# A graph network on one core: half-size stretches of the count matrix, one-hots of their own for the seam matmul, and the first block's counts fetched during the build

## The chip, the core and the metric

The kernel runs on 1 core of one Trainium2 chip. The metric is device time in microseconds (us). TensorE is called PE below, its weight loads PEld, VectorE DVE, ScalarE ACT, GpSimd POOL, and SyncE SP; a "q" behind the name (SPq, PEldq) marks that engine's own instruction sequencer, where DMA issues and register loads stand.

## The reference, cut to what matters

Two graph layers over 6250 nodes with 128 features and 200000 edges that are sorted by destination:

```python
h = jnp.maximum(_layernorm(x, axis=-1), 0.0)
# layer 0: agg_src = segment_sum(h[src], dst); agg_edge = segment_sum(edge_attr, dst)
x = x + relu(concatenate([h, agg_src, agg_edge], axis=1) @ W.T + b)
h = jnp.maximum(_layernorm(x, axis=-1), 0.0)
# layers 1 and 2 (mean over the neighbours, the same edges)
h1 = relu(mean(h[src]) @ W1_l + b1 + h @ W1_r)
out = x + relu(mean(h1[src]) @ W2_l + b2 + h1 @ W2_r)
```

## The kernel before

The kernel never gathers rows. It builds once a matrix `counts_d` in DRAM that says how many edges lead from each source node to each destination node, and then does each of the three layers as a dense matmul with it. Nodes are cut into NB = 49 blocks of 128; `counts_d` has 128 rows (source modulo 128), and for each destination node 49 bf16 columns (source block), so a destination block of 128 nodes is 12544 bytes a row, 1568 KB in all.

**The build.** Edges are taken in 196 groups of 1024, a group in 8 tiles of 128 edges. A tile's counts are a product of two one-hot matrices: `sp` (source modulo 128) stands, `sq` (destination place times 49 plus source block) moves. DVE writes both for a whole group by comparing an iota with an index (`onehots`, L391); PE multiplies (L504) into a PSUM tile `pu`; ACT copies the product into an SBUF buffer `ring` at a place that is read from a list (`to_put`, L531). Since edges are sorted, a tile touches a narrow window of `w` destination nodes. `REGIONS` says for each 14 groups: tiles per window `n`, window `w`, groups per stretch `k`, nodes of a stretch `sw`, window of the edge sums. Groups of one stretch share one `ring` buffer (three in rotation, each of SWMAX = 148 nodes, 14504 bytes a partition). At a stretch's end SP writes the whole ring to `counts_d` (L559) at a column that it reads from the list `first_i`; these writes overlap one another, and each is ordered behind the one before.

Where two windows meet they can share a node. For n > 1 (the first 84 groups) POOL adds the first 49 columns of a window to the ring (L534), and at the start of a stretch copies 49 columns over from the ring before (L481). For n = 1 (the last 112 groups, from group G1 = 84) PE does it: each tile's product gets a second matmul (L516) with the edges of the tile before, whose `sq` is read at an offset that a register holds:

```python
step = steps[t0 if t0 != live[0] else 0]
for j0, (sp_b, sq_b, t) in enumerate(last_tiles):
    mm = nc.tensor.matmul(pu[:, i * 512 : i * 512 + NB], sp_b[:, t, :],
                          sq_b[:, t, bass.ds(step, NB)], start=False, ...)
```

The 8 offsets of a group come from the list `step_i`, by one register load on PE's sequencer in each group (`group_values`, its load has the line L384); ACT loads its 8 places from `at_i` in the same way, once in each group.

Woven into this, PE sums the edges' features: `edge_sums` loads 512 KB of edges (SP, L403, three buffers), makes a one-hot `hot` (L405), multiplies (L414, fp32), and DVE adds the sum to `aggE` (L419) at a place read from `first_i`. The 196 edge groups are spread so that 1.27 of them fall on each group with n = 1. Every third group also gets one block of layer 0's linear part (`first_layer`), up to block 48.

**The layers.** When the build's pools are closed, 49 destination blocks follow for each layer (`neighbours`): SP loads the block's counts into `c` (L578, 1568 KB, three buffers in the pool `loads`, which takes the SBUF that the build had), PE runs 49 matmuls (L584), DVE reduces and finishes, ACT and PE make the next layer's terms (`next_layer`). For every second block DVE also takes the largest count (`high` L592, `worse` L593). `windows_right` tests on the fly that the windows held all edges: POOL loads the lists into `both`, `nexts` and `rows`, and DVE works over them (L642 to L689). In the program it is called from the second layer's loop.

The order of instructions on each engine is not the program's: a list scheduler chooses it ahead of the run, by the dependences and by its own estimate of durations. So work that nothing holds back, as these tests, can be moved far ahead.

Of the kernel before, what the change touches and what calls it, by code (L numbers as in the profile page):

```python
# [9 lines left out]
F32 = mybir.dt.float32  # L10
F16 = mybir.dt.float16
BF16 = mybir.dt.bfloat16
I32 = mybir.dt.int32
AF = mybir.ActivationFunctionType
ALU = mybir.AluOpType
AX = mybir.AxisListType
ET = mybir.EngineType
# [17 lines left out]

REGIONS = (
    (4, 4, 14, 40, 8),
    (4, 6, 14, 110, 12),
    (2, 5, 7, 100, 18),
    (2, 7, 7, 134, 22),  # L40
    (2, 8, 2, 60, 28),
    (2, 9, 2, 70, 32),
    (1, 6, 2, 74, 36),
    (1, 7, 2, 86, 42),
    (1, 8, 2, 98, 46),
    (1, 9, 2, 106, 52),
    (1, 10, 2, 118, 56),
    (1, 10, 2, 128, 62),
    (1, 11, 2, 140, 68),
    (1, 12, 2, 148, 74),  # L50
)
SWMAX = 148
WINMAX = 74


# [1 line left out]
def kernel(ctx: ExitStack, tc: tile.TileContext, x, srcl, dstl, edge, w0t, b0, w1l, b1, w1r, w2l, b2, w2r, out):  # L57
# [31 lines left out]
    for g0, g1, *reg in regions:  # L89
        for g in range(g0, g1, reg[2]):  # L90
            stretches.append((g, min(reg[2], g1 - g), *reg))
    NS = len(stretches)

    dram = ctx.enter_context(tc.tile_pool(name="dram", bufs=1, space=bass.MemoryType.DRAM))
    counts_d = dram.tile([P, (NP + SWMAX) * NB], BF16, name="counts_d")
# [25 lines left out]
    first = const.tile([P, 2, G], F32, name="first")  # L121
    terms = [keep.tile([P, NB, TW], BF16, name="terms0")]
    aggE = keep.tile([P, NP + WINMAX], F32, name="aggE")

    build = ExitStack()
    lists = build.enter_context(tc.tile_pool(name="lists", bufs=1))
# [3 lines left out]
    at_i = lists.tile([1, GC * U], I32, name="at_i")  # L130
    first_i = lists.tile([1, G], I32, name="first_i")
    G1 = next(g for g, _, n, *_ in stretches if n == 1)
    step_i = lists.tile([1, (G - G1) * U], I32, name="step_i")
    seam_i = lists.tile([1, NS], I32, name="seam_i")
    NQ = max(w for _, _, _, w, *_ in regions) * NB
    iota = lists.tile([P, NQ + NQ % 2], F16, name="iota")
# [140 lines left out]
    while si < NS:  # L277
# [21 lines left out]
    nc.vector.tensor_tensor(seam[:, 1:], seam[:, 1:], most[:, : NS - 1], op=ALU.min)  # L299
    nc.vector.tensor_scalar(seam, seam, 0.0, float(NB), op0=ALU.max, op1=ALU.mult)  # L300
    nc.vector.tensor_copy(seam_i, seam)
    steps = room.rearrange("o g u -> o (g u)")[:, : (G - G1) * U]
    nc.vector.tensor_tensor(steps, flat(unit)[:, G1 * U :], flat(unit)[:, G1 * U - 1 : GU - 1], op=ALU.subtract)
    nc.vector.tensor_scalar(
        steps, steps, float(max(r[3] for r in regions) - 1), float(NB), op0=ALU.min, op1=ALU.mult
    )
    nc.vector.tensor_scalar(step_i, steps, 0.0, None, op0=ALU.max)

    nc.sync.dma_start(unit_d[1 : GU + 1].unsqueeze(0), flat(unit))
    for end, u in ((0, 0), (GU + 1, GU - 1)):  # L310
# [4 lines left out]

    nc.vector.tensor_scalar(
        bad[:, 1:2], starts[:, NS - 1 : NS], -1.0, float(NC * P - stretches[-1][5]), op0=ALU.mult, op1=ALU.add
    )
    setup.close()
    nc.gpsimd.memset(terms[0][:, :, NK * D :], 1.0)  # L320
# [62 lines left out]
    def group_values(ap, engine, most):  # L383
        _, values = nc.values_load_multi_w_load_instructions(  # L384
            ap, engines=[engine], min_val=0, max_val=most, skip_runtime_bounds_check_because="clamped on the chip"
        )
        return values

    def onehots(to, index, n, m):
# [5 lines left out]
            op=ALU.is_equal,  # L395
        )

    def edge_sums(g):

        win = win_of(g)  # L400
        e = edges.tile([P, U, D], F32, name="edge_t")
        at_e = min(g * EG, E - EG)
        nc.sync.dma_start(e, edge[at_e : at_e + EG, :].rearrange("(p u) f -> p u f", u=U))  # L403
        hot = padded[g % len(padded)]
        nc.vector.tensor_tensor(  # L405
            hot[:, :, :win],
            iota[:, :win].unsqueeze(1).to_broadcast([P, U, win]),
            rel[:, g, :].unsqueeze(2).to_broadcast([P, U, win]),
            op=ALU.is_equal,
        )  # L410
        ps = bpsum.tile([P, 512], F32, name="pe", bufs=2)
        for u in range(U):
            behind = yield
            mm = nc.tensor.matmul(ps[:, :P], e[:, u, :], hot[:, u, :], start=u == 0, stop=u == U - 1)  # L414
            if behind is not None:
                tc.add_manual_dep(mm.ins, behind.name, IN_ORDER, reason="in turn with the counts")
        base = value(first_i[0:1, g : g + 1], ET.DVE, N - 1)
        to = aggE[:, bass.ds(base, win)]
        nc.vector.tensor_tensor(to, to, ps[:, :win], op=ALU.add)  # L419

    def all_edge_sums():
        for g in range(G):
            yield from edge_sums(g)

    edge_tiles = all_edge_sums()
    next(edge_tiles)
# [40 lines left out]
    before = None  # L467
    counted = None
    writes = []
    steps_of = {}  # L470
    block = 0
    for i in range(2):
        load_chunk(i)
    for si, (g0, ng, n, w, k, sw, win) in enumerate(stretches):
# [4 lines left out]
        if before is not None and n > 1:  # L479
            v = value(seam_i[0:1, si : si + 1], ET.Pool, (SWMAX - 1) * NB)  # L480
            nc.gpsimd.tensor_copy(ring[:, :NB], before[:, bass.ds(v, NB)])  # L481
        for g in range(g0, g0 + ng):
            sp = hots.tile([P, U, P], BF16, name="sp")
            onehots(sp, p_e[:, g], U, P)
            even = nq + nq % 2
# [4 lines left out]
            if n > 1:  # L490
                to_add = group_values(places, ET.Pool, (sw - w) * NB)
            else:
                steps = steps_of.pop(g)
            live = [t for t in range(0, U, n) if g < G - 1 or (t + n) * P > unused]
            many = 2 if nq <= 512 else 1
            for j in range(0, len(live), many):
                units = live[j : j + many]
                pu = bpsum.tile([P, 2 * 512], F32, name="pu", bufs=3)
                for i, t0 in enumerate(units):
                    for t in range(t0, t0 + n):  # L500
                        c = i * 512
                        while c < i * 512 + nq:
                            z = min(c // 512 * 512 + 512, i * 512 + nq)
                            mm = nc.tensor.matmul(  # L504
                                pu[:, c:z],
                                sp[:, t, :],
                                sq[:, t, c - i * 512 : z - i * 512],
                                start=t == t0,
                                stop=t == t0 + n - 1 and (n > 1 or c > i * 512),
                            )  # L510
                            c = z
                    if n == 1:

                        step = steps[t0 if t0 != live[0] else 0]
                        for j0, (sp_b, sq_b, t) in enumerate(last_tiles):
                            mm = nc.tensor.matmul(  # L516
                                pu[:, i * 512 : i * 512 + NB],
                                sp_b[:, t, :],
                                sq_b[:, t, bass.ds(step, NB)],
                                start=False,  # L520
                                stop=j0 == len(last_tiles) - 1,
                            )
                    last_tiles = [(sp, sq, t) for t in range(t0, t0 + n)]
                if n > 1:
                    fore = small.tile([P, 2, NB], F32, name="fore", bufs=8)
                    nc.scalar.copy(  # L526
                        fore[:, : len(units), :], pu.rearrange("p (i c) -> p i c", c=512)[:, : len(units), :NB]
                    )
                for i, t0 in enumerate(units):
                    if n == 1:  # L530
                        nc.scalar.copy(ring[:, bass.ds(to_put[t0], nq)], pu[:, i * 512 : i * 512 + nq])  # L531
                        continue
                    to = ring[:, bass.ds(to_add[t0 // n], NB)]
                    add = nc.gpsimd.tensor_tensor(to, to, fore[:, i, :], op=ALU.add)  # L534
                    tc.add_to_no_dep_group(f"add{si}", add.ins)
                    put = nc.scalar.copy(  # L536
                        ring[:, bass.ds(to_put[t0 // n] + NB, nq - NB)], pu[:, i * 512 + NB : i * 512 + nq]
                    )

                    tc.declare_no_dep(put.ins, group=f"add{si}", reason="a later window's other nodes stand behind it")  # L540
                spent += share(n) * len(units) / len(live)
                sum_edges(min(int(spent / shares * GU + 0.5), GU), counted)
                counted = mm.ins
                if j == 0 and G1 <= g + 1 < G:

                    steps_of[g + 1] = group_values(
                        step_i[0:1, (g + 1 - G1) * U : (g + 2 - G1) * U], ET.PE, (max(r[3] for r in regions) - 1) * NB
                    )

            if len(writes) > 1 or block == NB and writes:  # L550
                writes.pop(0)()
# [5 lines left out]
        else:  # L557
            begin = value(first_i[0:1, g0 : g0 + 1], ET.SP, N - 1) * NB
        nc.sync.dma_start(counts_d[:, bass.ds(begin, sw * NB)], ring[:, : sw * NB])  # L559
        before = ring  # L560
    assert block == NB and summed == GU and not writes
    build.close()
# [9 lines left out]
    def neighbours(layer, b):  # L572
# [1 line left out]
        ps = psum.tile([P, 512], F32, name="ps", bufs=3)  # L574
        m = NK * D + (layer == 0)
        products = []
        c = loads.tile([P, P, NB], BF16, name="c")
        nc.sync.dma_start(c, counts_d[:, b * P * NB : (b + 1) * P * NB].rearrange("p (d k) -> p d k", k=NB))  # L578
        for k in range(NB):
            products.append((c[:, :, k], terms[layer % 2][:, k, :m]))  # L580
        for i, (stands, moves) in enumerate(products):
# [26 lines left out]
    def windows_right():  # L608

        both = late.tile([P, 2, GU], F32, name="both")  # L610
        dst, far = both[:, 0], both[:, 1]
        nc.gpsimd.dma_start(dst.bitcast(I32), dstl)
        nexts = late.tile([P, GU], I32, name="nexts")
        nc.gpsimd.memset(nexts[P - 32 :, GU - U :], PAD)
        nc.gpsimd.dma_start(nexts[: P - 1, :], dstl[1:, :])
        nc.gpsimd.dma_start(nexts[P - 1 :, : GU - U], dstl[0:1, U:])
# [361 lines left out]
```

## Time and profile before

| | us |
|---|---|
| median of 3 runs (2259.93 to 2263.4) | 2262.35 |
| the profiled execution: its own time | 2267.7 |
| the profiled execution: span from first to last instruction | 2266.0 |
| busy: PE / DVE / ACT / POOL | 2067.5 / 1207.9 / 791.9 / 217.9 |
| stage with n > 1 | about 48 to 319 |
| stage with n = 1 | 319 to 934 |
| first matmul of layer 0 | 947.16 |
| layers 0, 1, 2 | 947 to 1405, to 1850, to 2266 |

The mean granted clock of TensorE was 0.982. Busy time is the union of an engine's instructions; the ends of matmuls are modelled, so small gaps of PE are not all seen. "Idle before" names what ended the idle time of an engine; "issue" means that nothing the profile follows ended it, and a register load on the engine's own sequencer is such a case.

### The profile page before, as it was taken

To read this page: it belongs to the slowest core of one execution; us is meant where nothing else is said; L and a number is where in the kernel's file an instruction comes from. 1 tells how busy PE (TensorE), PEld (TensorE's weight loads), DVE (VectorE), ACT (ScalarE), POOL (GpSimd) and SP (SyncE) were. 2 spreads that over 40 slices of the span, in tenths; PEclk is the share of its full clock that TensorE was granted. 3 is DMA by queue.
4 is the path that set the end of the run, shared out by engine and by line. 5 is a ranking of instruction groups with operands and counts; after the bars stand their busy time and mean duration, and the time that the engine had idled before them with its cause. 6 is when DMAs were issued, how large, how long until landed. Compare 5 with 4: busy or idle time off the path is not lost.

```text
span 2266.0 us, 39466 instructions
## 1 busy us (share of the span) xinstructions
PE 2067.5 (91%) x13713; PEld 1693.1 (75%) x13713; DVE 1207.9 (53%) x2296; ACT 791.9 (35%) x2010; POOL 217.9 (10%) x421
## 2 busy tenths in 40 slices
PE   6977778898888888779999999999999999999998
PEld 5865557777666666567888887778888888888887
DVE  8987765677666666475555555444444431111111
ACT  3565566788888787311111111111111110000000
POOL 5666650000000000100000000000000000000000
PEclk9999999999999999899999999999999999999999
DMA  3554566777777677745555555555555556666663
GB/s 116 187 170 166 187 222 227 254 273 263 250 254 266 243 257 258 271 157 205 209 204 202 200 199 196 180 192 186 191 204 191 185 200 218 228 227 229 226 226 135
DMA packets 140315, 478.93 MB, mean 211 GB/s; under 512 B 15249, under 2 KB 85967, under 8 KB 114384
## 3 DMA queue, kind: packets, MB, share of 16 engines
q1 hardware_dynamic: 81540, 447.53, 55.5%
q10 hardware_dynamic: 57996, 27.16, 4.2%
q8 instruction: 115, 1.88, 0.3%
q0 software_dynamic: 576, 1.63, 0.2%
q14 instruction: 88, 0.72, 0.1%
HBM read 362.19 MB, written 114.08 MB: 210 GB/s over the span
## 4 chain that ended last, share of the span: by engine, by line
PE 61%; issue 10%; DVE 10%; DMA 9%; ACT 6%; ACTq 2%; POOLq 1%; POOL 1%; DVEq 0%; SPq 0%
PE ps L584 37%; PE pe L414 12%; PE pu L504 7%; DMA c<-counts_d 6%; ACT ring L531 3%; PE pz L344 2%; DVE high L592 2%; DVE sq L391 1%; DVE worse L593 1%; PE pu L516 1%; ACTq L384 1%; DMA edge_t<-in_edge 1%; PE pt L341 1%; ACT ring L536 1%; ACT h L334 1%
## 5 line engine op out<-in xcount | busy, mean ns | idle before, releaser
L584 PE MATMUL ps<-terms,c 128*128 128x384 bf16 (+1 forms) x7203 | 1228.3, 327 | 13.1 <-DMA c<-counts_d 13.1
L584 PEld LDWEIGHTS <-c 128*128 128x128 bf16 x7203 | 1020.5, 142 | 180.6 <-issue 18.8
L414 PE MATMUL pe<-hot,edge_t 128*128 128x128 f32 x3136 | 517.9, 294 | 19.9 <-DMA edge_t<-in_edge 12.8
L531 ACT CAST ring<-pu 128x490 f32 (+6 forms) x891 | 470.3, 534 | 108.2 <-PE pu L516 69.9
L414 PEld LDWEIGHTS pe<-hot,edge_t 128*128 128x128 f32 x3136 | 419.0, 195 | 78.6 <-issue 32.3
L504 PE MATMUL pu<-sq,sp 128*128 128x512 bf16 (+7 forms) x1782 | 396.3, 315 | 34.1 <-ACT ring L536 16.1
L391 DVE TENSOR_TENSOR sq<-iota,q_e 128x3136 bf16<-128x3136 f16 (+8 forms) x196 | 353.2, 1802 | 0.0
L595 DVE TENSOR_REDUCE y<-ps 128x128 f32<-128x384 f32 x147 | 81.2, 553 | 384.7 <-PE ps L584 384.7
L504 PEld LDWEIGHTS <-sp 128*128 128x128 bf16 x1782 | 176.3, 100 | 140.5 <-issue 84.2
L391 DVE TENSOR_TENSOR sp<-iota,p_e 128x1024 bf16<-128x1024 f16 x196 | 136.2, 695 | 172.3 <-PE pu L516 154.8
L516 PE MATMUL pu<-sq,sp 128*128 x892 | 163.5, 186 | 64.4 <-issue 63.6
L534 POOL TENSOR_TENSOR ring<-ring,fore 128x49 f32 x280 | 173.5, 620 | 89.9 <-ACT fore L526 30.3
L593 DVE TENSOR_REDUCE worse<-high 128x1 f32<-128x3136 bf16 x49 | 167.5, 3419 | 1.6
L347 DVE TENSOR_TENSOR r<-pz,b_sb 128x128 f32<-128x128 f32 x98 | 28.6, 292 | 226.8 <-ACT terms L345 226.8
L536 ACT CAST ring<-pu 128x196 f32 (+5 forms) x280 | 112.0, 404 | 71.9 <-issue 34.9
L330 ACT ACTIVATE rstd<-mv,eps 128x1 f32<-128x1 f32 x98 | 29.0, 300 | 287.2 <-DVE mv L328 287.2
L516 PEld LDWEIGHTS <-sp 128*128 128x128 bf16 x892 | 87.4, 98 | 43.2 <-issue 12.6
L732 ACT ACTIVATE h<-y 128x128 f32<-128x128 f32 x49 | 15.1, 309 | 289.4 <-DVE y L724 289.4
L592 DVE TENSOR_TENSOR high<-c 128x3136 bf16<-128x3136 bf16 x49 | 87.7, 1790 | 49.4 <-DMA c<-counts_d 49.1
L405 DVE TENSOR_TENSOR hot<-iota,rel 128x64 f32<-128x64 f16 (+13 forms) x196 | 96.0, 492 | 0.6 <-POOL hot L375 0.6
L350 ACT CAST terms<-z 128x128 bf16<-128x128 f32 x147 | 44.0, 300 | 92.9 <-DVE z L349 92.1
L351 DVE TENSOR_TENSOR terms<-z,terms 128x128 bf16<-128x128 f32 x147 | 44.2, 301 | 59.6 <-ACT terms L350 59.3
(138 smaller groups left out, 820.7 us busy)
## 6 DMA issues: line engine op xcount, KB each, us to landing
c<-counts_d SPq DMA_DIRECT2D x147, 1568.0 KB, 6.4
edge_t<-in_edge SPq DMA_DIRECT2D x196, 512.0 KB, 3.7
counts_d<-ring SPq DMA_DIRECT2D x7, 1813.0 KB, 6.2
counts_d<-ring SPq DMA_DIRECT2D x7, 1715.0 KB, 6.5
counts_d<-ring SPq DMA_DIRECT2D x7, 1568.0 KB, 6.7
counts_d<-ring SPq DMA_DIRECT2D x7, 1445.5 KB, 5.7
own<-r_d ACTq DMA_DIRECT2D x147, 64.0 KB, 5.5
counts_d<-ring SPq DMA_DIRECT2D x7, 1298.5 KB, 6.2
```

What stands on the lines that cost most here:

```text
L391: nc.vector.tensor_tensor(to.rearrange("p t (c two) -> p t c two", two=2), iota[:, :m].rearrange("p (c two) -> p c two", two=2).unsqueeze( ...
L405: nc.vector.tensor_tensor(hot[:, :, :win], iota[:, :win].unsqueeze(1).to_broadcast([P, U, win]), rel[:, g, :].unsqueeze(2).to_broadcast([P ...
L414: mm = nc.tensor.matmul(ps[:, :P], e[:, u, :], hot[:, u, :], start=u == 0, stop=u == U - 1)
L504: mm = nc.tensor.matmul(pu[:, c:z], sp[:, t, :], sq[:, t, c - i * 512 : z - i * 512], start=t == t0, stop=t == t0 + n - 1 and (n > 1 or c ...
L516: mm = nc.tensor.matmul(pu[:, i * 512 : i * 512 + NB], sp_b[:, t, :], sq_b[:, t, bass.ds(step, NB)], start=False, stop=j0 == len(last_tile ...
L531: nc.scalar.copy(ring[:, bass.ds(to_put[t0], nq)], pu[:, i * 512 : i * 512 + nq])
L534: add = nc.gpsimd.tensor_tensor(to, to, fore[:, i, :], op=ALU.add)
L536: put = nc.scalar.copy(ring[:, bass.ds(to_put[t0 // n] + NB, nq - NB)], pu[:, i * 512 + NB : i * 512 + nq])
L584: nc.tensor.matmul(ps[:, :m], stands, moves, start=i == 0, stop=i == len(products) - 1)
L592: nc.vector.tensor_tensor(high, cf[:, :half], cf[:, half:], op=ALU.max)
L593: nc.vector.tensor_reduce(worse[:, 6 + b : 7 + b], high, AX.X, ALU.max)
L595: nc.vector.tensor_reduce(y, ps[:, : NK * D].rearrange("p (k f) -> p f k", k=NK), AX.X, ALU.add)
```

## The change

Four things are done.

The stretches get shorter. In regions 1, 2 and 3 a stretch has 7, 4 and 3 groups in place of 14, 7 and 7, and in the last six regions 1 group in place of 2; `sw` goes down with it and SWMAX from 148 to 86. The number of stretches, and so of ring writes, goes from 76 to 124.

The seam matmul of n = 1 gets one-hots of its own. `carries` works out once, at group 14, an index `carry` for each tile (the index of the edges less the step); for each group DVE writes `sc` from it, 9 tiles of 50 columns at most, and L516 reads `sc` at a fixed place. The register load of `step_i` on PE is gone.

A buffer `c_early` (12544 bytes a partition) is kept from the start. POOL loads block 0's counts into it for layer 0 once all but the last 6 stretches are written; a further entry of `bad` tests that those 6 do not reach block 0. In the layers, each fourth block (b % 4 == 0) uses `c_early` and no buffer of `loads`.

The tests of the lists are tied to layer 0: POOL copies a column of `rdeg` of block 12 into `dst`, and one of block 16 into `nexts`, before it loads them.

```diff
 REGIONS = (
     (4, 4, 14, 40, 8),
-    (4, 6, 14, 110, 12),
-    (2, 5, 7, 100, 18),
-    (2, 7, 7, 134, 22),
+    (4, 6, 7, 70, 12),
+    (2, 5, 4, 62, 18),
+    (2, 7, 3, 66, 22),
     (2, 8, 2, 60, 28),
...
-    (1, 8, 2, 98, 46),
-    (1, 9, 2, 106, 52),
-    (1, 10, 2, 118, 56),
-    (1, 10, 2, 128, 62),
-    (1, 11, 2, 140, 68),
-    (1, 12, 2, 148, 74),
+    (1, 8, 1, 54, 46),
+    (1, 9, 1, 60, 52),
+    (1, 10, 1, 68, 56),
+    (1, 10, 1, 72, 62),
+    (1, 11, 1, 76, 68),
+    (1, 12, 1, 82, 74),
 )
-SWMAX = 148
+SWMAX = 86
...
+    EARLY = NS - 6
...
+    c_early = keep.tile([P, P, NB], BF16, name="c_early")
...
+    nc.vector.tensor_scalar(
+        bad[:, 3:4], starts[:, EARLY : EARLY + 1], -1.0, float(P), op0=ALU.mult, op1=ALU.add
+    )
...
+    def carries():
+        ones = small.tile([1, P], F32, name="ones", bufs=1)
+        nc.vector.memset(ones, 1.0)
...
+        for i in range(2):
+            nc.tensor.matmul(
+                pu[:, i * 512 : i * 512 + half], ones, steps[:, i * half : (i + 1) * half], start=True, stop=True
+            )
+            nc.vector.tensor_tensor(
+                carry[:, 1 + i * half : 1 + (i + 1) * half],
+                flat_q[:, T1 - 1 + i * half : T1 - 1 + (i + 1) * half],
+                pu[:, i * 512 : i * 512 + half].unsqueeze(2).to_broadcast([P, half, 2]),
+                op=ALU.subtract,
+            )
...
         for g in range(g0, g0 + ng):
+            if g == RUN:
+                carries()
...
             else:
-                steps = steps_of.pop(g)
+                of_first = 2 if g == G1 else 1
+                sc = hots.tile([P, U + 1, NB + NB % 2], BF16, name="sc")
+                c0 = g * U - T1 + 1
+                onehots(
+                    sc[:, 2 - of_first : U + 1], carry[:, c0 + 1 - of_first : c0 + U], U + of_first - 1, NB + NB % 2
+                )
...
-                                sq_b[:, t, bass.ds(step, NB)],
+                                sc[:, slot + 1 - len(last_tiles) + j0, :NB],
...
-                if j == 0 and G1 <= g + 1 < G:
-                    steps_of[g + 1] = group_values(
-                        step_i[0:1, (g + 1 - G1) * U : (g + 2 - G1) * U], ET.PE, (max(r[3] for r in regions) - 1) * NB
-                    )
...
         nc.sync.dma_start(counts_d[:, bass.ds(begin, sw * NB)], ring[:, : sw * NB])
+        if si == EARLY - 1:
+            load_counts(nc.gpsimd, c_early, 0)
...
-        c = loads.tile([P, P, NB], BF16, name="c")
-        nc.sync.dma_start(c, counts_d[:, b * P * NB : (b + 1) * P * NB].rearrange("p (d k) -> p d k", k=NB))
+        c = c_early if b % 4 == 0 else loads.tile([P, P, NB], BF16, name="c")
+        if b or layer:
+            load_counts(nc.sync, c, b)
...
+        nc.gpsimd.tensor_copy(dst[:, 0:1], rdeg[:, 12:13])
         nc.gpsimd.dma_start(dst.bitcast(I32), dstl)
         nexts = late.tile([P, GU], I32, name="nexts")
+        nc.gpsimd.tensor_copy(nexts[:, 0:1], rdeg[:, 16:17])
```

More of the change, by code (lines that the diff above doesn't have):

```diff
@@ L132 @@
     G1 = next(g for g, _, n, *_ in stretches if n == 1)
-    step_i = lists.tile([1, (G - G1) * U], I32, name="step_i")
+    T1 = G1 * U
+    carry = lists.tile([P, GU - T1 + 1, 2], F16, name="carry")
+    steps = lists.tile([1, GU - T1], F32, name="steps")
     seam_i = lists.tile([1, NS], I32, name="seam_i")
@@ L301 @@
     nc.vector.tensor_copy(seam_i, seam)
-    steps = room.rearrange("o g u -> o (g u)")[:, : (G - G1) * U]
-    nc.vector.tensor_tensor(steps, flat(unit)[:, G1 * U :], flat(unit)[:, G1 * U - 1 : GU - 1], op=ALU.subtract)
+    nc.vector.tensor_tensor(steps, flat(unit)[:, T1:], flat(unit)[:, T1 - 1 : GU - 1], op=ALU.subtract)
     nc.vector.tensor_scalar(
-        steps, steps, float(max(r[3] for r in regions) - 1), float(NB), op0=ALU.min, op1=ALU.mult
+        steps, steps, float(max(r[3] for r in regions)), float(NB), op0=ALU.min, op1=ALU.mult
     )
-    nc.vector.tensor_scalar(step_i, steps, 0.0, None, op0=ALU.max)
     nc.sync.dma_start(unit_d[1 : GU + 1].unsqueeze(0), flat(unit))
@@ L396, in onehots @@
         )
+    def carries():
+        ones = small.tile([1, P], F32, name="ones", bufs=1)
+        nc.vector.memset(ones, 1.0)
+        flat_q = q_e.rearrange("p g u two -> p (g u) two")
+        pu = bpsum.tile([P, 2 * 512], F32, name="pu", bufs=3)
+        half = (GU - T1) // 2
+        assert half <= 512 and 2 * half == GU - T1
+        for i in range(2):
[8 more added lines that the diff above has]
+            )
+        nc.vector.tensor_tensor(
+            carry[:, 0:1], flat_q[:, T1 - 2 : T1 - 1], pu[:, 0:1].unsqueeze(2).to_broadcast([P, 1, 2]), op=ALU.subtract
+        )
     def edge_sums(g):
@@ L423, in all_edge_sums, with load_counts @@
             yield from edge_sums(g)
+    def load_counts(queue, c, b):
+        queue.dma_start(c, counts_d[:, b * P * NB : (b + 1) * P * NB].rearrange("p (d k) -> p d k", k=NB))
     edge_tiles = all_edge_sums()
@@ L469 @@
     writes = []
-    steps_of = {}
     block = 0
@@ L492 @@
             else:
-                steps = steps_of.pop(g)
+                of_first = 2 if g == G1 else 1
[3 more added lines that the diff above has]
+                    sc[:, 2 - of_first : U + 1], carry[:, c0 + 1 - of_first : c0 + U], U + of_first - 1, NB + NB % 2
+                )
             live = [t for t in range(0, U, n) if g < G - 1 or (t + n) * P > unused]
@@ L512 @@
                     if n == 1:
-                        step = steps[t0 if t0 != live[0] else 0]
-                        for j0, (sp_b, sq_b, t) in enumerate(last_tiles):
+                        slot = t0 + 1 if t0 != live[0] else 1
+                        for j0, (sp_b, t) in enumerate(last_tiles):
                             mm = nc.tensor.matmul(
@@ L522 @@
                             )
-                    last_tiles = [(sp, sq, t) for t in range(t0, t0 + n)]
+                    last_tiles = [(sp, t) for t in range(t0, t0 + n)]
                 if n > 1:
```

## The prediction

> **What bounds the kernel now.** I read the busy rows by stage first, then the waits of the stage that the change rewrites, then single instructions inside it, and last the passage from the build to layer 0. In the layers (947 to 2266 us) PE is the bound: between 1100 and 2266 it is busy for 1143.5 of 1166 us, so little can be gained there. The idle time is in the build. By region of 14 groups (last region, and the sum over the last six; columns: length, then busy time and count of PE, PEld, DVE, ACT, POOL, then clock, DMA share, GB/s):
>
> ```profile
> 848.00:934.10 86.10, 73.51 (x598) 57.20 (x596) 54.38 (x58) 69.17 (x108) 3.12 (x1) 0.98 0.68 246
> sum 472.60, PE 412.39 PEld 322.52 DVE 315.60 ACT 385.81 POOL 3.33; mean PE 68.73 PEld 53.75 DVE 52.60 ACT 64.30 POOL 0.55
> ```
>
> Those 84 groups take 5.63 us each, and PE is idle for 60.2 of the 472.6 us. The waits of 319 to 934 say where (engine, line, what it waited for: total us, times, longest):
>
> ```profile
> DVE sp L391 <- PE pu L516: 154.8, 93, 4.6
> ACT ring L531 <- PE pu L516: 69.9, 89, 2.1
> ...
> PE pu L516 <- issue: 63.6, 65, 2.8
> ```
>
> PE stops before the seam matmul L516 with nothing visible to wait for, and ACT and DVE then stop for PE. What stands there is the register load of `step_i`. Two group ends in a row, with SP's issues around them:
>
> ```profile
> L384 PEldq TENSOR_LOAD <-step_i x1: 1697/1697/1697, 804.5 to 804.5; - x1
> L384 ACTq TENSOR_LOAD <-at_i x1: 1626/1626/1626, 805.2 to 805.2; - x1
> ```
>
> ```profile
> L384 ACTq TENSOR_LOAD <-at_i x1: 547/547/547, 810.9 to 810.9; - x1
> L384 PEldq TENSOR_LOAD <-step_i x1: 589/589/589, 810.9 to 810.9; - x1
> ```
>
> ```profile
> 800.63 0.35 SPq L559 DMA_DIRECT2D counts_d<-ring  x1
> 803.92 5.89 SPq L403 DMA_DIRECT2D edge_t<-in_edge  x2
> 813.07 0.35 SPq L559 DMA_DIRECT2D counts_d<-ring  x1
> ```
>
> The loads at 804.5 and 805.2 fall 4 to 6 us after a ring write was issued, and take 1.7 and 1.6 us; those at 810.9 have no write in flight and take 0.59 and 0.55. Writes of this size land late, so every second group end is a slow one:
>
> ```profile
> counts_d<-ring SPq DMA_DIRECT2D x7, 1813.0 KB, 6.2
> ...
> counts_d<-ring SPq DMA_DIRECT2D x7, 857.5 KB, 4.2
> ```
>
> Then the passage (start, length, engine, line, and in brackets the idle time before it):
>
> ```profile
> 947.16 0.51 PE L584 MATMUL ps<-terms,c 128*128 128x385 bf16 x1 [13.09 <-DMA c<-counts_d]
> ...
> 975.47 0.48 PE L341 MATMUL pt<-ident,h 128*128 128x128 f32 x1 [9.38 <-ACT h L334]
> ```
>
> ```profile
> 953.96 0.98 DVE L642 CAST both<-both 128x1568 f32<-128x1568 int32 x1 [19.61 <-DMA both<-in_dst]
> ```
>
> PE waits 13.1 us for block 0's counts, and later 9.4 us for block 0's result, because DVE stands in a list test whose load has not landed.
>
> **The change part by part**, against the profiled execution (2267.7 us, 5.3 above the median of 2262.35).
>
> *Register load of PE and shorter stretches: -36.* The ceiling in the last six regions is PE's idle time, 60. It cannot all come back. ACT still loads `at_i`; a load of 0.55 us hides under the copy that runs (0.61), one of 1.6 to 2.2 does not. A ring of 82 nodes is 1004.5 KB; between the two DMA rows it lands in about 4.5 us, so a write issued at a group's start is down before ACT's next load some 5 us later. It is not always issued there: of the two writes above the second came 1.4 us late. I let 3 groups in 10 stay slow with 1.2 us exposed, half of it absorbed by the PSUM buffers: 84 x 0.3 x 1.2 / 2 = 15. A further quarter of the 60 I leave to edges and first-layer work, which become the next late thing: 15. That gives 30. The two regions that keep 2 groups a stretch have PE idle for 18.4 us; their load stays exposed for less, 6. Ends: -66, and a loss if the writes set the pace (rival 1).
>
> [...]
>
> *One-hots `sc`: 0.* 450 columns: from the `sp` row (1024 columns, 692 ns) and the `sq` row (2352 columns, 1383 ns), 0.52 ns a column, so 0.39 us, 112 times: 44 us on DVE. They hide in the 154.8 us that DVE waits for L516; without that cover they cost up to 44.
>
> *`carries`: +2* (0 to 4). Two fp32 matmuls of 448 columns (3.5 times the 0.27 us of an edge tile) and two subtractions of 896 columns (1568 cost 1.79 us, so 1.0 each). DVE is busy for 35.4 of 36 us there, so its 2 us count.
>
> *Six more seams with n > 1, with their POOL copies and SP's writes: +4* (0 to 8). In 48 to 319 PE waited 11.9 us for edge loads that stood behind ring writes on SP, over 18 seams: 0.65 each. For nothing at all speaks that the region with w = 9 and 7 stretches (50 us) is no slower than that with w = 7 and 2 stretches (53).
>
> *`c_early` in the build: +4* (0 to 10). POOL issues it (0.8 us) after write 189 has landed; it reads 1568 KB, 6.4 us by the `c` row, 12.5 by the POOL load of `both`. Write 190 overlaps the range as far as can be known ahead, so it must wait for the read. Behind it on SP stand the edge loads, issued some 9 us ahead and landing in 3.7 to 7.3, and the next ring writes; behind the read on POOL stands the last ring's memset (3.1 us, now 1.8).
>
> *Passage: -18.* Block 0 can begin about 1 us after the last edge sum and lasts 8.6. Block 1's counts: last write landed at +4.7 (smaller than before), load 7.1 like the first `c` now, so +11.8; today block 1 starts at +21.3. That is 9.5; the hole of 9.4 goes too if DVE is free. Less 1 for waits that stay.
>
> *List tests after block 12: +4* (0 to 12). Some 14 us of DVE work (the rows from L642 to L689) into layer 0, where DVE is free for 44% of the time. What can cost is again a test placed ahead of its load: that of `both` took 12.5 us. Queued behind the two new copies on POOL are only the list loads and a memset for block 48.
>
> *Fourth counts buffer: +2.* Blocks 48 and the next layer's 0 use `c_early` back to back: if PE takes block 0 first, it stands for a load (6.4 us) at both layer ends, up to 14; if block 1 goes first, nothing: +4. An earlier load for the rest: DVE waits 49.1 us for `c` in its count tests, PE hardly: -2 (0 to -10).
>
> Sum: -36 + 0 + 2 + 4 + 4 - 18 + 4 + 2 = -38, so 2229.7 on the profiled execution's scale and 2224 on the median's.
>
> **The rivals.**
> 1. *The writes set the pace (slower).* Each write waits for the one before to land: one landed at 331.46 and the next went out at 331.60. With one write a group, a group cannot be shorter than landing plus 0.35 us of issue. It decides from 5.63 - 0.35 = 5.3 us. Against: 735 KB lands in 3.9, 857.5 in 4.2. For: 1053.5 KB took 6.2 and 1445.5 KB 5.7, behind edge loads on the same engines. [...] At 5.7 us: 84 x 6.05 = 508, +36 in place of -30, total +28: about 2290 (2264 to 2310). Also, a write would then be in flight at every ACT load.
> [...]
> 3. *Covers fail:* DVE becomes the bound with `sc`, or the costs in the layers and around `c_early` stand at their upper ends (48 in place of 16): -36 - 18 + 48 = -6, 2256; with 40 us of `sc` in the open, 2264.
> 4. *The tests do not move usefully:* a test stands ahead of its load at block 12 as it did at block 0; the hole of 9.4 only moves. 2233, inside the main case.
>
> **How the numbers follow.** Main case 0.51 (2204 to 2246, rival 4 included), rival 2 0.19, rival 1 0.21, rival 3 0.09 (a third faster, half the same, the rest slower). About 0.2% (4.5 us) is what a measurement of this kernel can tell from no change. Faster: 0.51 + 0.18 + 0.03 = 0.72; same 0.05; slower 0.23. The range leaves out the upper part of rival 1 (0.14) and a low tail of 0.05.
>
> **What would show it.** Right: no load of `step_i`, L516 without idle time before it, ACT's `at_i` loads near 0.55 us in the last regions, the build's end 30 us earlier, layer 0 begun within 2 us of it. Wrong: ring writes that wait for landings, `edge_t` among PE's releasers, an idle PE where layers 1 and 2 begin.

## The result: slower by 0.4%, and the profile after

| | kernel before | changed kernel |
|---|---|---|
| median of 20 runs each, us | 2258.38 (2251.01 to 2265.65) | 2267.73 (2262.02 to 2275.51) |
| ratio to before, 95% interval | | 1.0039 (1.0028 to 1.0051) |
| the profiled execution, us | 2267.7 | 2263.15 |

The forecast was 0.983 of the median that it knew; the kernel became slower. One thing first: the two profiled executions stand the other way round. That of before lies above all of its 20 runs, that of the changed kernel near the lowest of its own. So the traces tell here where time went, and only the ratios over many runs tell how much.

The n = 1 stage got shorter. From the first to the last ring copy of the stage, before and after (length, busy time of PE, PEld, DVE, ACT, POOL, clock, DMA share, GB/s):

```profile
319.80:934.10 614.30, 535.97 (x4340) 426.94 (x4339) 402.21 (x635) 488.15 (x990) 7.45 (x10) 0.98 0.72 254
```

```profile
324.80:925.20 600.40, 541.40 (x4322) 421.35 (x4321) 434.04 (x748) 486.53 (x994) 4.84 (x7) 0.99 0.77 274
```

PE's idle time in the stage falls from 78 to 59 us, DVE's work grows by 32. The row of the seam matmul (the last two fields are the idle time before it and its releaser) has lost its wait, and the waits of 319 to 934 have changed hands:

```profile
L554 PE MATMUL pu<-sc,sp 128*128 128x49 bf16 x892 | 162.5, 186 | 0.0
```

```profile
ACT ring L569 <- PE pu L554: 41.4, 48, 3.2
PE pu L542 <- ACT ring L569: 36.7, 51, 8.6
ACT ring L569 <- DMA counts_d<-ring: 20.9, 14, 8.9
```

The same wait of PE for ACT's copies stood in the kernel before as

```profile
PE pu L504 <- ACT ring L531: 5.2, 16, 0.6
```

and so 5.2 us have become 36.7. And one wait of 8.6 is new. It stands at the end of the build, where `c_early` is read. SP's issues there, then PE's matmuls with idle time in front, in order of time through the passage and the two layer ends:

```profile
889.56 0.35 SPq L592 DMA_DIRECT2D counts_d<-ring  x1
890.01 8.77 SPq L431 DMA_DIRECT2D edge_t<-in_edge  x3
905.90 4.30 SPq L592 DMA_DIRECT2D counts_d<-ring  x2
```

```profile
910.50 0.65 PE L542 MATMUL pu<-sq,sp 128*128 128x512 bf16 x2 [8.63 <-ACT ring L569]
...
925.36 0.36 PE L620 MATMUL ps<-terms,c_early 128*128 128x385 bf16 x1 [0.42 <-DVE aggE L447]
942.17 0.48 PE L346 MATMUL pt<-ident,h 128*128 128x128 f32 x1 [8.29 <-ACT h L339]
...
961.72 0.47 PE L346 MATMUL pt<-ident,h 128*128 128x128 f32 x1 [4.86 <-ACT h L339]
...
1411.44 0.48 PE L346 MATMUL pt<-ident,h 128*128 128x128 f32 x1 [7.44 <-ACT h L339]
...
1859.17 10.86 PE L620 MATMUL ps<-terms,c_early 128*128 128x384 bf16 x49 [3.39 <-DMA c_early<-counts_d]
```

Read from the top: ring writes that went out every 5.6 us (in the mean of 844 to 890) stop for 16 us, the ring buffers run out, and ACT and then PE stand (8.6). Layer 0 does begin at once (0.4 us of wait in place of 13.1). Then PE stands 8.3 us for block 0's result and 4.9 for the next; and at the ends of layers 0 and 1 it stands 7.4 and 3.4 us, where the kernel before had two holes of 2.8 and 2.4, and nothing. The 8.3 have their cause in DVE's own order:

```profile
936.27 1.79 DVE L628 TENSOR_TENSOR high<-c_early 128x3136 bf16<-128x3136 bf16 x1 [0.48 <-POOL nothing L678]
...
938.10 3.42 DVE L629 TENSOR_REDUCE worse<-high 128x1 f32<-128x3136 bf16 x1
941.43 0.15 DVE L337 SCALAR_TENSOR_TENSOR rstd<-mv,rstd 128x1 f32<-128x1 f32 x1
```

Block 0's own count test (5.2 us) sits between the statistics of its result and the last step of its norm. Such tests already stood there in the kernel before, where the prediction saw the list tests alone. From 953.96 on, up to the norm of block 0, DVE did two count tests, 10.4 us, beside the list tests; their second steps lie on both sides of block 0's sum `y`:

```profile
960.63 3.41 DVE L593 TENSOR_REDUCE worse<-high 128x1 f32<-128x3136 bf16 x1
...
967.88 0.54 DVE L595 TENSOR_REDUCE y<-ps 128x128 f32<-128x384 f32 x1
...
968.41 3.39 DVE L593 TENSOR_REDUCE worse<-high 128x1 f32<-128x3136 bf16 x1
```

### The profile page after: what moved, and what is told of

Same layout as the page of the kernel before. It is cut to its first block, busy times and chain, and to the rows that moved or that the text cites. A ratio compares the mean times of both kernels' runs of the same rounds, so it can differ in the third digit from the quotient of the medians.

```text
span 2261.4 us, 38810 instructions
## 1 busy us (share of the span) xinstructions
PE 2081.7 (92%) x13717; PEld 1692.3 (75%) x13717; DVE 1242.7 (55%) x2420; ACT 790.8 (35%) x2011; POOL 200.4 (9%) x430
## 4 chain that ended last, share of the span: by engine, by line
PE 53%; issue 13%; ACT 12%; DMA 12%; DVE 6%; ACTq 2%; POOL 0%; POOLq 0%; DVEq 0%; SPq 0%
PE ps L620 37%; ACT ring L569 10%; PE pe L442 6%; PE pu L542 5%; DMA counts_d<-ring 4%; DMA c<-counts_d 4%; DMA edge_t<-in_edge 2%; PE pz L349 2%; ACTq L389 2%; DVE high L628 1%; DVE worse L629 1%; DMA c_early<-counts_d 1%; DVE sq L396 1%; PE pt L346 1%; PE pu L349 1%
## 5 line engine op out<-in xcount | busy, mean ns | idle before, releaser
L620 PE MATMUL ps<-terms,c 128*128 128x384 bf16 (+1 forms) x5292 | 907.4, 327 | 0.0
L620 PEld LDWEIGHTS <-c 128*128 128x128 bf16 x5292 | 749.7, 142 | 122.7 <-issue 3.5
L542 PE MATMUL pu<-sq,sp 128*128 128x512 bf16 (+7 forms) x1782 | 391.3, 315 | 67.9 <-ACT ring L569 36.7
L620 PE MATMUL ps<-terms,c_early 128*128 128x384 bf16 (+1 forms) x1911 | 334.5, 329 | 3.8 <-DMA c_early<-counts_d 3.4
L620 PEld LDWEIGHTS <-c_early 128*128 128x128 bf16 x1911 | 270.8, 142 | 51.8 <-issue 5.4
L572 POOL TENSOR_TENSOR ring<-ring,fore 128x49 f32 x280 | 159.4, 569 | 110.8 <-ACT fore L564 40.3
L554 PE MATMUL pu<-sc,sp 128*128 128x49 bf16 x892 | 162.5, 186 | 0.0
L628 DVE TENSOR_TENSOR high<-c 128x3136 bf16<-128x3136 bf16 x36 | 64.4, 1790 | 44.9 <-DMA c<-counts_d 44.9
## 6 DMA issues: line engine op xcount, KB each, us to landing
counts_d<-ring SPq DMA_DIRECT2D x14, 1004.5 KB, 4.8
```

Source lines behind the costliest of these rows:

```text
L542: mm = nc.tensor.matmul(pu[:, c:z], sp[:, t, :], sq[:, t, c - i * 512 : z - i * 512], start=t == t0, stop=t == t0 + n - 1 and (n > 1 or c ...
L620: nc.tensor.matmul(ps[:, :m], stands, moves, start=i == 0, stop=i == len(products) - 1)
L628: nc.vector.tensor_tensor(high, cf[:, :half], cf[:, half:], op=ALU.max)
```

## The experiments

The theory after the result: the build gained, and the gain was lost again to `c_early`, in the build, at the passage and above all at the layer ends. The rival: the short, ordered ring writes lose what the one-hots gain. Ratios are to the kernel before, run beside each. Traces of one and the same build differ, too: the n = 1 stage took 590, 596 and 600 us in e6_po, e4_no_early and e11_noearly_clear, whose programs are alike up to the layers.

| run | short stretches | one-hots | c_early | ratio (95%) |
|---|---|---|---|---|
| e1_onehots | last region only | yes | no | 0.9966 (0.9952 to 0.9980) |
| e2_short | yes | no | no | 0.9951 (0.9935 to 0.9968) |
| e6_po | yes | yes | no | 0.9932 (0.9909 to 0.9955) |
| e4_no_early | yes | yes | no, tests tied | 0.9934 (0.9911 to 0.9957) |
| the changed kernel | yes | yes | each 4th block | 1.0039 (1.0028 to 1.0051) |
| e7_rotate | yes | yes | rotating | 0.9984 (0.9973 to 0.9994) |
| e3_early_once | yes | yes | block 0 of layer 0 | 0.9953 (0.9939 to 0.9967) |
| e8_sooner | yes | yes | the same, loaded at group 88 | 0.9943 (0.9924 to 0.9962) |
| e9_clear | yes | yes | the same, DVE cleared | 0.9936 (0.9915 to 0.9957) |
| e10_all | yes | yes | both repairs | 0.9899 (0.9881 to 0.9917) |
| e11_noearly_clear | yes | yes | no, DVE cleared | 0.9935 (0.9910 to 0.9959) |

**Own one-hots alone (e1_onehots).**

```diff
-    (1, 12, 2, 148, 74),
-SWMAX = 148
+    (1, 12, 1, 82, 74),
+SWMAX = 140
...
-                                sq_b[:, t, bass.ds(step, NB)],
+                                sc[:, slot + 1 - len(last_tiles) + j0, :NB],
```

> The kernel before with one part of the change alone: the seam matmul reads one-hots of its own (sc), so PE's register load is gone. Stretches stay at two groups in the last regions, except in the very last region (1 group), where the room for the new buffers comes from. No c_early, tests not tied. Theory A (the register load of PE was worth real time; what the whole change lost, it lost elsewhere): n = 1 stage shorter by 15 to 30 us, 2230 to 2245. Theory B (ACT's own slow register loads and copies hold the group's pace anyway, so PE's load was covered): within 6 us of the kernel before, 2252 to 2264.

It took 2252.5 us where the kernel before took 2260.0: between the two theories, 7.5 us for taking the load off PE (with one region of short stretches, and with DVE's work on `sc` as its price). The load was largely covered: in place of the load, PE now waits for ACT, 44.6 us where it was 5.2:

```profile
PE pu L538 <- ACT ring L565: 44.6, 63, 1.7
```

**Short stretches alone (e2_short).** REGIONS and SWMAX as in the changed kernel, nothing else.

> The kernel before with the short stretches alone (REGIONS and SWMAX of the changed kernel); PE still loads its steps, no c_early, tests not tied. Theory A (a ring write in flight is what makes register loads slow, and shorter writes are down in time): the loads of step_i and at_i in the last six regions fall to about 0.6 us, n = 1 stage shorter by 10 to 25 us; n > 1 stage longer by about 7; sum 2240 to 2256. Theory B (the ordered writes set the pace and SP's edge loads stand behind them): n = 1 stage not shorter, sum 2262 to 2275.

2248.9 us, 11 less than before; theory A in the time, though its 7 us more for n > 1 did not come (278 us in both traces). The loads of `step_i` in the last six regions, before and then here (min/median/max in ns):

```profile
L384 PEldq TENSOR_LOAD <-step_i x83: 587/883/2950, 464.6 to 928.9; - x83
```

```profile
L384 PEldq TENSOR_LOAD <-step_i x83: 587/594/2054, 463.7 to 915.5; - x83
```

The median falls to 0.59, near the lowest, but many loads stay slow: 36 of the 83 still take over 0.8 us, where it was 43, and PE still stands before L516 for 45.6 us in place of 63.6:

```profile
PE pu L516 <- issue: 45.6, 66, 1.7
```

That the slow loads are those behind a ring write can be read from the trace of before, load by load. Of its 83, the 42 that began within 5 us of a write's issue all took 0.88 us or more, 1.86 in the mean; the 41 others took 0.61 in the mean and 0.82 at most, though for 38 of them an edge load had gone out less than 3.7 us before. So these edge loads did not do it.

The rival is out. Writes do wait for each other much more often; these are SP's waits for an earlier landing, before and in the changed kernel:

```profile
SPq L559 <- DMA counts_d<-ring: 17.6, 12, 3.5
```

```profile
SPq L592 <- DMA counts_d<-ring: 97.3, 68, 4.9
```

But these waits pass on SP. ACT stood 17.4 us for ring writes in e2_short's n = 1 stage, and the kernel is faster all the same. The two gains overlap: 7.5 and 11 us alone, 15 together (e6_po).

**Both, without c_early (e4_no_early), and without the tie of the list tests as well (e6_po).**

```diff
-        if si == EARLY - 1:
-            load_counts(nc.gpsimd, c_early, 0)
...
-        c = c_early if b % 4 == 0 else loads.tile([P, P, NB], BF16, name="c")
-        if b or layer:
-            load_counts(nc.sync, c, b)
+        c = loads.tile([P, P, NB], BF16, name="c")
+        load_counts(nc.sync, c, b)
```

> The changed kernel without c_early: block 0's counts are loaded by SP after the build, three buffers in plain rotation. Theory A (c_early costs more than it brings: 8.6 us of idle PE at the end of the build, about 7 at the two layer ends, against 12.6 saved at the passage): within 5 us of the changed kernel, 2260 to 2270, with the passage at 12 us again and no idle PE over 3 us at the layer ends. Theory B (c_early pays, the loss is in the short stretches): 12 us slower than the changed kernel, 2275 or more.

> The changed kernel without c_early and without the two copies that tie the list tests to blocks 12 and 16: short stretches and own one-hots alone. Against the run without c_early (0.9934 of the kernel before) this takes out the tie alone. Theory A (tying the tests frees the first blocks of layer 0): the wait of DVE for both and a hole of 8 us or more in PE before the first transpose come back; 3 to 8 us slower than that run, ratio 0.995 to 0.997. Theory B (the tests cost as much at block 12 as at block 0): within 2 us of it.

Neither theory of the first had it: without `c_early` the kernel is 1.05% faster than with it (0.9934 against 1.0039, some 24 us), and faster than before. I had counted 8.6 and about 7 us against it and 12.6 for it. And e6_po gives the same ratio, theory B: tying the tests is worth nothing that intervals of 5 us to each side could show. In e6_po the hole before the first transpose is 7.6 us and in e4_no_early 2.8; the latter pays in later blocks of layer 0, with four holes over 0.7 us up to 1130, 6.7 us together, where e6_po has one of 1.7.

**Which use of c_early costs (e7_rotate, e3_early_once).**

```diff
-        c = c_early if b % 4 == 0 else loads.tile([P, P, NB], BF16, name="c")
+        c = c_early if (layer * NB + b) % 4 == 0 else loads.tile([P, P, NB], BF16, name="c")   # e7_rotate
+        c = c_early if b == 0 and layer == 0 else loads.tile([P, P, NB], BF16, name="c")       # e3_early_once
```

> The changed kernel with the fourth buffer in plain rotation: c_early serves each block whose running number (layer times 49 plus block) is a multiple of 4, so that block 48 and the next layer's block 0 no longer share it. Theory A (the loss is the back-to-back use at the two layer ends, and the clock that PE loses after it stood still): PE has no wait for c at the layer ends, 14 to 20 us faster than the changed kernel, 2244 to 2254. Theory B (a fourth buffer disturbs the blocks inside the layers): less than 6 us faster.

> The changed kernel, with c_early used for block 0 of layer 0 only; all other blocks rotate through the three buffers of loads. Theory A (back-to-back use of c_early by block 48 and the next layer's block 0 costs at both layer ends): 5 to 9 us faster than the changed kernel, 2259 to 2263, and no wait of PE for c at the start of layer 2. Theory B (the fourth buffer helps within the layers as much as it costs at their ends): within 3 us of the changed kernel.

Plain rotation takes 0.55% away, about 12 us, a little less than theory A's 14 to 20: the back-to-back use at the layer ends is the largest single loss. The 40 us around each end, in the changed kernel and then in e7_rotate (PE's busy time is the second number, its matmuls stand in brackets):

```profile
1400.00:1440.00 40.00, 32.20 (x175) 24.87 (x174) 13.39 (x28) 4.46 (x15) 0.00 (x0) 0.87 0.40 141
1840.00:1880.00 40.00, 34.93 (x192) 27.05 (x191) 6.51 (x20) 2.28 (x8) 0.00 (x0) 0.91 0.42 147
```

```profile
1400.00:1440.00 40.00, 34.52 (x186) 26.40 (x185) 18.97 (x38) 4.94 (x16) 0.00 (x0) 0.91 0.40 141
1840.00:1880.00 40.00, 40.00 (x240) 33.32 (x239) 7.48 (x21) 3.42 (x12) 0.00 (x0) 1.00 0.58 207
```

The changed kernel does 59 matmuls fewer, at 0.17 us each about 10 us (an estimate from these rows). 48 of them are missing at the end of layer 1, where its shorter stall stands. There PE waits for the load of `c_early`, and e7_rotate stands not at all. The 7.4 us at the end of layer 0 are another wait: the row names ACT's `h`. Block 0's counts can be loaded only after block 48's last matmul, so PE has no matmuls of the next block to do while block 48's result is made, behind a count test of 5.2 us on DVE. e7_rotate has such matmuls, but it stands near that place too, 3.1 and 2.1 us for two other results.

Using the buffer once takes away another 0.31%, 7 us: as a fourth buffer inside the layers it does harm, not good. (Both together are 19 us; e3_early_once's theory A had 5 to 9.) Layer 0's first 16 blocks take some 170 us in e7_rotate's trace and 163 in e3_early_once's. The traces name a part of that. In the changed kernel SP issues block 4's load into `c_early` at 946.98, 0.5 us ahead of a tiny load of the list tests, `rows<-nothing`. That one then takes 5.7 us to land (1.5 in the kernel before, where SP had issued no load of counts in the 15 us ahead of it). DVE waits for it, with block 1's result behind, and so comes the hole of 4.9 us (3.9 in e7_rotate). The wait in the changed kernel, and in e3_early_once, which has no such hole:

```profile
953.28 0.26 DVE L728 TENSOR_REDUCE worse<-rows 14x1 f32<-14x112 f32 x1 [4.39 <-DMA rows<-nothing]
```

```profile
955.68 0.26 DVE L728 TENSOR_REDUCE worse<-rows 14x1 f32<-14x112 f32 x1 [0.23 <-DMA rows<-nothing]
```

No run moved this load alone, and the rest of the 7 us is open.

Why a stall of 7.4 us costs more than itself is seen around the end of layer 0, in the changed kernel and in e3_early_once (25 us each; PE's busy time is the second number, the clock the third from the end):

```profile
1395.00:1420.00 25.00, 17.03 (x84) 12.00 (x82) 10.34 (x25) 3.23 (x10) 0.00 (x0) 0.80 0.43 150
```

```profile
1395.00:1420.00 25.00, 22.55 (x131) 17.89 (x130) 11.88 (x29) 3.98 (x13) 0.00 (x0) 0.98 0.49 165
```

The granted clock is 0.80 against 0.98: after it stood, PE ran part of the next block slowly, and did 84 matmuls where the other did 131. Finer windows of the changed kernel show the slow stretch itself:

```profile
1407.30:1417.40 10.10, 5.60 (x16) 2.97 (x17) 3.79 (x13) 1.62 (x5) 0.00 (x0) 0.50 0.28 107
1417.50:1427.60 10.10, 10.10 (x62) 8.35 (x61) 1.39 (x4) 1.13 (x4) 0.00 (x0) 1.00 0.32 108
```

For ten us the clock was 0.50, and PE worked for 5.6 of them. The matmuls of L620 start 0.32 us apart in the first of these rows and 0.165 in the second (medians), so the stall cost some 2.8 us beyond its length (an estimate from these numbers). At the end of layer 1 the clock was 0.50 for 6.6 us with PE busy for 5.3, and the same matmuls start 0.32 us apart.

**The two stalls of c_early (e8_sooner, e9_clear, e10_all), and the clearing without it (e11_noearly_clear).**

```diff
-    EARLY = NS - 6
+    EARLY = next(i for i, s in enumerate(stretches) if s[0] >= 6 * RUN + 4)    # e8_sooner
...
-        if b % 2 == layer:
+        if (b % 2 == layer) if b else layer == 1:                              # e9_clear
...
+        nc.gpsimd.tensor_copy(rows[:, :, 0], rdeg[:NR, 16:20])                 # e9_clear
```

> The run with c_early for layer 0's block 0 only (0.9953), with its load moved from the sixth stretch before the end to group 88, where a stretch still has two groups and lasts some 10 us. Theory A (the read holds the next ring write, and the short stretches of the end can't take that): the 8 us of idle PE near the end of the build is gone, 5 to 9 us faster than that run, ratio 0.991 to 0.993. Theory B (the stall only moves to group 88): within 2 us of that run.

> The run with c_early for layer 0's block 0 only (0.9953), with two things taken out of the way of block 0's result: the largest count of block 0 is taken in layer 1 in place of layer 0, and the load of rows for the list tests is tied to blocks 16 to 19 as well. Theory A (DVE's tests stand between block 0's sums and its result): the hole of 8.3 us in PE before the first transpose shrinks below 2 us, 6 to 9 us faster than that run with the clock it saves, ratio 0.991 to 0.993. Theory B (PE would stand at that place for the counts of block 1 or 2 anyway): less than 3 us faster.

> c_early for layer 0's block 0 only, loaded at group 88, block 0's largest count taken in layer 1, rows tied as well: both repairs together. Theory A (the two stalls are separate and add up): passage of 1 us, no stall at the end of the build, first hole in layer 0 below 3.5 us; 10 us faster than with neither (0.9953), ratio 0.989 to 0.992. Theory B (c_early brings nothing net, whatever is mended): 0.993 to 0.995, as without it.

> Short stretches and own one-hots, no c_early, tests tied to blocks 12 and 16 with rows tied too, block 0's largest count taken in layer 1. Theory A (the first hole of layer 0 is DVE's tests): passage 17 us, first hole below 2 us, ratio 0.989 to 0.992. Theory B (without c_early the hole is covered by the wait for counts anyway, and the tests cost as much later): 0.992 to 0.995.

In the traces each repair does what it should. e8_sooner has no stall near the end of the build. e9_clear has a first hole of 3.3 us (I expected below 2), and its stall in the build is still there:

```profile
918.63 0.65 PE L542 MATMUL pu<-sq,sp 128*128 128x512 bf16 x2 [8.59 <-ACT ring L569]
933.54 0.36 PE L620 MATMUL ps<-terms,c_early 128*128 128x385 bf16 x1 [0.42 <-DVE aggE L447]
945.31 0.47 PE L346 MATMUL pt<-ident,h 128*128 128x128 f32 x1 [3.26 <-ACT h L339]
```

In time, neither alone can be told from e3_early_once (2 and 4 us, the intervals overlap), and neither came to its theory A. Both together can: 0.9899 against 0.9953, 12 us, theory A. Without `c_early` the clearing brings nothing (0.9935), theory B: there PE waits 16.1 us for block 0's counts, and DVE has time to test. e10_all is the fastest version of this study, 1.0% below the kernel before and 1.4% below the changed one; its interval touches those of the runs without `c_early` (0.9909 to 0.9955 for e6_po), so that the early load pays once it is mended is likely and not quite certain.

**What holds the n = 1 stage now (e12_act_half, e13_no_hot).**

```diff
-                        nc.scalar.copy(ring[:, bass.ds(to_put[t0], nq)], pu[:, i * 512 : i * 512 + nq])
+                        nc.scalar.copy(ring[:, bass.ds(to_put[t0], nq // 2)], pu[:, i * 512 : i * 512 + nq // 2])   # e12
...
-        nc.vector.tensor_tensor(hot[:, :, :win], ...)
+        if g < 56:
+            nc.vector.tensor_tensor(hot[:, :, :win], ...)                      # e13
```

> Short stretches and own one-hots alone (the run at 0.9932), with ACT copying only the first half of each product of the n = 1 groups into the ring; the other half of the counts is left out, so the layers work with wrong counts in the same time. Theory A (after the register load of PE is gone, ACT's copies hold the pace of the n = 1 stage): PE's waits for ACT's ring copies vanish, the stage is 15 to 35 us shorter, ratio 0.978 to 0.987. Theory B (what is left is DVE's one-hots, edge loads and the ordered ring writes): less than 6 us, ratio above 0.990.

> Short stretches and own one-hots alone (the run at 0.9932), with DVE's one-hots of the edges left out from edge group 56 on (the buffers hold zeros or earlier one-hots, so those edge sums are wrong): about 0.9 us less of DVE work in each n = 1 group, everything else the same. Theory A (ACT holds the pace, DVE has slack in spite of sc): within 5 us of that run, ratio 0.991 to 0.995. Theory B (DVE, with the 44 us of sc, is the next bound): 15 us faster or more, ratio below 0.987.

With copies of half the width, ACT is busy for 327 us of the stage in place of 486: 0.9813 (0.9798 to 0.9829), 27 us below e6_po. Some 65 us, 15%, of DVE's work less in the stage: 0.9904 (0.9888 to 0.9921), 6 us, the intervals overlapping. So ACT is what the stage waits for once PE's load is gone, and DVE matters little. Theory A of e12_act_half has its time but not its sign: PE's waits for ACT's copies did not vanish (32.2 us, in e6_po 27.9), and in its trace the stage takes 581 us, 9 to 18 less than in the three traces with whole copies, so that a part of the 27 is not seen there. With half copies the ordered ring writes come to the front, and ACT stands for them:

```profile
ACT ring L565 <- DMA counts_d<-ring: 112.0, 58, 4.8
...
ACT ring L565 <- PE pu L550: 77.8, 157, 3.3
...
PE pu L538 <- ACT ring L565: 32.2, 32, 3.4
```

## Why the prediction was wrong

Three terms failed, by 17, 15 and 15 us: forecast +2, -10 and -30, measured +19, +5 and -15. The measured ones are steps of one chain of runs and add up to +9, which is what the kernel lost.

**The step that failed by most: "Fourth counts buffer: +2".** It saw the place (blocks 48 and 0 share `c_early`, 4 us, up to 14) and took a gain of 2 for the rest. The runs show 12 us for the back-to-back use (e7_rotate) and 7 more for the fourth buffer itself (e3_early_once): 19 in place of 2. Three things were missed. PE's order is the scheduler's choice, and I gave block 1 first a good chance; block 0 came first at both ends. I priced a stall by its length alone, where ten us at a clock of 0.50 cost some 2.8 us more (and 2.7 at the other end, estimates from the rows above). And I gave the earlier loads of a fourth buffer a gain of 2 and no cost, where behind one of them a list test's load landed late (5.7 us against 1.5 in the kernel before), and block 1's result with it.

**"Passage: -18" with "`c_early` in the build: +4" and "List tests: +4".** Together -10. Measured with `c_early` used once, against e6_po: 0.9953 to 0.9932, about +5, intervals overlapping. The 13.1 us at the start of layer 0 did go. The hole of 9.4 did not. I had put it down to a list test whose load was late, but two count tests, 10.4 us, stood in the same place, and tying the list tests left block 0's own count test there (a hole of 8.3 us); besides, only the lists `both` and `nexts` had been tied, not `rows`. The ring writes stood for the read as described, at the upper end (8.6 of the 10 allowed). With both mended the once-used buffer is 12 us faster (e10_all), of the 15 that were missing.

**"Register load of PE and shorter stretches: -36", "carries", "seams": together -30.** Measured alone (e6_po): 0.9932, -15. The mechanism held: in the last six regions of the kernel before, loads within 5 us of a ring write's issue were slow (42 of 42, 0.88 us or more) and the 41 others short (0.82 at most), and shorter writes alone bring 11 us (e2_short). That halving the writes pays nothing by itself, as the chance of 0.19 for rival 2 has it, no run shows. The size was off by half. I left 15 us to slow loads and 15 to edges, and the main case did not use how much of a group ACT's copies fill. These copies in the last region of the kernel before (busy us, mean ns, then the idle time before them):

```profile
L531 ACT CAST ring<-pu 128x588 f32 x107 | 69.3, 652 | 17.4 <-PE pu L516 14.3
```

Eight copies of 0.652 us are 5.2 of the 6.15 us of a group there (86.10 over 14). e12_act_half shows what held the rest back: 27 us come free when ACT copies less.

**What held.** `sc` hides (e13_no_hot: DVE is not the bound). Rival 1 did not decide: 1004.5 KB land in 4.8 us in the changed kernel and in 5.5 in e6_po (4.5 estimated, 5.3 needed), and yet with short stretches alone the kernel is faster; smaller writes moved fewer bytes a us (1004.5 KB in 4.8 us are 209 KB a us; before, 1813 KB landed in 6.2, 292) and cost no time. Rival 4's picture, a hole that only moves, was right: the list test of `both` makes one of 4.0 us at 1086. Rival 3 came nearest: it set the costs in the layers and around `c_early` at their upper ends and named them as what could eat up the gain, but it stopped at 6 us faster. And the prediction's own sign of being wrong, an idle PE where layers 1 and 2 begin, is what came.

## What to carry to other kernels

Where one buffer of a rotation is pinned to fixed indices, look at the wrap-around: the last index of one pass and the first of the next must not share it. A prefetch that reads what later writes may touch makes these writes wait (here for 16 us, and PE stood for 8.6 of them); put it where the writes have slack. And before counting a removed stall on one engine as time, add up the other engines' work per period in the same stretch: the smallest slack among them is what can be gained.

## What the runs showed of the hardware that I had not expected

In the last six regions of the kernel before, a register load of 8 values from SBUF (TENSOR_LOAD of `step_i` on PE's sequencer) took 0.59 to 0.82 us, and 0.88 to 2.95 when a write from SBUF to DRAM had been issued in the 5 us before it; of the 41 short ones 38 had an edge load from DRAM into SBUF issued less than 3.7 us before. PE stood for 7.4 us at the end of layer 0, to 1411.4 us; from 1407.3 to 1417.4 the granted clock was 0.50, and the matmuls started 0.32 us apart in place of 0.165. A tiny load took 5.7 us in the changed kernel, where one of 1568 KB had gone out 0.5 us ahead of it, and 1.5 in the kernel before, where none had in 15 us. Executions of one kernel spread by 15 us (2251 to 2266), and a single profiled one can lie outside that.
